# Layer 0 of a conv-attention kernel: rows in blocks of 1024 by single key tiles, doubled keys, and an output projection in four quadrants of the array

## The chip, the cores and the metric

The kernel runs on one core of one Trainium2 chip. The core has five engines that run side by side, each with its own queue in program order: TensorE (matrix products, PE in the profile, its weight loads PEld), VectorE (DVE), ScalarE (ACT), GpSimd (POOL) and SyncE (SP), from which most DMA transfers are issued. Engines wait for each other by semaphores. TensorE writes to PSUM[...]; the other operands lie in SBUF.

The metric is the device time of one launch, in microseconds, the median of several runs. Less is better. A profiled execution has a span, from its first to its last instruction; the time of a run is a little more than the span.

## The reference

The input x is 4 images of 128 channels and 64x64 places, so 4 batches of N = 4096 tokens of 128 channels. Two layers follow each other:

```
# layer 0, per batch; xf is (128, 4096), m = 64
q, k, v = wq @ xf, wk @ xf, wv @ xf          # each (64, 4096)
att = softmax(k.T @ q, axis=2)               # 4096 x 4096, no mask
x = x + wo @ (att @ v.T).T                   # residual

# layer 1 on tokens t (4096, 128)
h = layernorm(t)
q, k, v = h @ Wq, h @ Wk, h @ Wv             # 128 wide
t = t + softmax(causal(q @ k.T / sqrt(128))) @ v
# then a recurrent feed-forward step over tokens, with a norm, added to t
```

All arithmetic is in float32. The change lies in layer 0; layer 1 matters because it follows layer 0 of the same batch and shares engines and buffers with it.

## The kernel before

**Sizes.** P = 128, BLK = 512 rows (NB = 8 blocks a batch), TPB = 4 tiles of 128 in a block, NT = 32 key tiles, M = 64, B = 4 batches.

**Items.** The attention of both layers is one list of items (`items`), in the order batch, layer, block, pair of key tiles. "Rows" are what the softmax is taken for; "keys" are the other side. For each item `scores` multiplies keys by rows into `s_ps` (128 keys on partitions, two tiles of 512 rows side by side) and ScalarE takes the exp into `p`; `sums` adds `p` to `dsum` on VectorE (the denominators, still spread over partitions); `values` multiplies `v` by `p` and accumulates in `acc` over the block. There are two `s_ps` buffers, four `p` buffers and one `acc`. Values follow scores by two items (`SKEW`), so TensorE alternates: scores of item s, values of item s-2.

**Layer 0 before.** An item is two key tiles, t and t+16, for one block of 512 rows, 16 items a block and 128 a batch. The contraction is only 64 long, so each product uses a quarter of TensorE's array: tile t from partitions 0 to 63, tile t+16 from 64 to 127, and each in two halves of 64 keys. The four run at once. For this the rows of a block must lie on both halves of the partitions: `cols0` projects block m and block m+4 into `kr` (q on one half of the partitions, k on the other) and copies the k half to the other partitions, into `swap`, by DMA. `values` does likewise: partitions 0 to 63 of `acc` get the sum over tiles t, partitions 64 to 127 that over t+16, in two banks for the two halves of the keys in a tile.

When a block ends (`it.last`), ScalarE copies `acc` to `half`, VectorE adds its two banks to `agg` (kept in `xhT`), still with two partial sums on the two halves of the partitions; VectorE adds the two halves of `dsum` to `den`.

**Leaving layer 0.** A block's `agg` is not projected at once but at a visit. At the end of the blocks named in `visits`, `leave` issues the output projection `o_ps` on TensorE: four products 128x128x128 a block with `wo2`, which holds wo twice, so that the contraction over 128 partitions also adds the two partial sums. Then a chain of steps, each due some items later, follows: `joined` (four `xs` on VectorE: o_ps times the reciprocal denominator plus the residual), `moments` (statistics of the layernorm), `norm` and `by_channels` (VectorE transposes, then transfers through DRAM that bring the block into channel layout, `xhT`). The chain of denominators (`folded`: VectorE transpose `sq`, reduction `part`, a transfer through DRAM; then `denominators`) starts at the block's end. All chains wait in one list, and one step is done per item; layer 1's chains wait in the same list.

```
visits = [{2: (0, 1), 4: (2, 3), 6: (4,), 7: (5,)}, {2: (6,), 3: (7,)}]
```

This reads: after block 2 of layer 0 the blocks 0 and 1 leave, after 4 the blocks 2 and 3, after 6 block 4, after 7 block 5; after blocks 2 and 3 of layer 1 the blocks 6 and 7.

**The pool "m".** `misc` hands out PSUM banks from a pool of two buffers (`ps_m`). The output projections `o_ps` of both layers take from it, and so do the projected rows of layer 1 (`r_ps`, in `rows1`), the keys and values of the next batch (`kr_ps`, `v_ps`), and others. A buffer comes free when the last reader of its tile is done; for `o_ps` that is the fourth `xs` of `joined`. At the end of a block `rows()` prepares the rows of the block after next: in layer 0 this takes no instruction, in layer 1 it is an `r_ps`. Before the change `rows()` stands ahead of the visit's projections.

**Order.** The program is written in the order above, and a scheduler then orders each engine's instructions by its own estimates of when they are ready. What comes out is a fixed order on each engine; a waiting instruction holds back all that stand behind it on its engine.

In layer 1, two key tiles of 128x128 products make an item, blocks of 512 rows are causal (block g has 2g+2 items), and the array is used whole. Going from products of 64 rows to products of 128 and back is thus what happens around each `o_ps` and `r_ps` in layer 0.

Of the kernel before, what the change touches and what calls it, by code (L numbers as in the profile page):

```python
# [15 lines left out]
P = 128  # L16
# [343 lines left out]
def fast_path(  # L360
# [63 lines left out]
    for m in range(NB // 2):  # L424
        for g in (m, m + NB // 2):
            nc.sync.dma_start(out=xs[:, 0, ts(g, BLK)], in_=x[0, :, ts(g, BLK)])
# [55 lines left out]
    with tc.tile_pool(name="batch", bufs=1) as batch, tc.tile_pool(name="rows", bufs=2) as rowp, tc.tile_pool(  # L482
# [41 lines left out]
        def cols0(b, m):  # L524

            bt = bs[b]
            if m == 0:
                bt.kr = batch.tile([P, 2, N // 2], F32, tag="kr", name="kr")  # L530
                bt.swap = batch.tile([P, N // 2], F32, tag="swap", name="swap")
                bt.v = batch.tile([P, NT // 2, 2, M], F32, tag="v", name="v0")
            for h, w in enumerate((wqk, wkq)):
                ps = misc("kr_ps")
                nc.tensor.matmul(ps, lhsT=w, rhs=xs[:, b, ts(m + h * NB // 2, BLK)], start=True, stop=True)  # L535
                if h:
                    nc.scalar.copy(bt.kr[:, h, ts(m, BLK)], ps)
                else:
                    nc.vector.tensor_copy(bt.kr[:, h, ts(m, BLK)], ps)
                rows, keys = slice(M - h * M, P - h * M), slice(h * M, h * M + M)  # L540
                nc.sync.dma_start(out=bt.swap[keys, ts(m, BLK)], in_=bt.kr[rows, h, ts(m, BLK)])

        def vals0(b, m):

            ps = misc("v_ps")
            for h in range(2):
                nc.tensor.matmul(  # L547
                    ps[h * M : h * M + M], lhsT=wv0, rhs=xs[:, b, ts(m + h * NB // 2, BLK)], start=True, stop=True
                )
            if b:  # L550

                sq = wk.tile([P, Q * TPB, S], F32, tag="sqv", name="sqv")
                nc.vector.transpose(
                    out=sq.rearrange("p (q j) r -> p q j r", q=Q), in_=ps.rearrange("p (j q t) -> p q j t", q=Q, t=S)
                )
                by_t = dram2.tile([S, Q, TPB, Q, S], F32, tag="by_t", name="by_t")
                for c in range(Q):
                    nc.sync.dma_start(out=by_t[:, :, :, c].rearrange("t q j r -> t (q j) r"), in_=sq[ts(c, S)])
                for q in range(Q):
                    nc.sync.dma_start(  # L560
                        out=bs[b].v[ts(q, S), ts(m, TPB)].rearrange("t j h c -> t (j h c)"),
                        in_=by_t[:, q].rearrange("t j c r -> t (j c r)"),
                    )
                return
            vT = wk.tile([P, BLK], F32, tag="vT", name="vT")
            nc.scalar.copy(vT, ps)
            return vT
# [7 lines left out]
        def rows0(b, g):  # L575

            h, m = g // (NB // 2), g % (NB // 2)
            bt = bs[b]
            half = [bt.swap, bt.swap]
            half[1 - h] = bt.kr[:, h]  # L580
            bt.next.append([half[i][i * M : i * M + M, ts(m, BLK)] for i in range(2)])
# [56 lines left out]
        def projected(layer, agg):  # L638

            op = misc("o_ps")  # L640
            for j in range(TPB):
                nc.tensor.matmul(  # L642
                    op[:, ts(j, P)], lhsT=agg[:, ts(j, P)], rhs=wv1 if layer else wo2, start=True, stop=True
                )
            return op

# [72 lines left out]
        def finish0(b, g):  # L719

            agg, den = bs[b].agg, bs[b].den
            mem = []

            def norm():
                if g == 0:
                    bs[b].xh = batch.tile([P, NT, P], F32, tag="xh", name="xh")
                normed(b, g, bs[b].xh[:, ts(g, TPB)], *mem.pop())

            def by_channels():
                sq = squares(bs[b].xh[:, ts(g, TPB)])  # L730
                by_r = dram2.tile([S, Q, TPB, Q, S], F32, tag="by_r", name="by_r")
                for q in range(Q):
                    nc.sync.dma_start(
                        out=by_r[:, :, :, q].rearrange("r c j t -> r (c j) t"),
                        in_=sq[ts(q, S)].rearrange("r c j t -> r (c j) t"),
                    )
                for c in range(Q):
                    nc.sync.dma_start(
                        out=bs[b].xhT[ts(c, S), ts(g, BLK)], in_=by_r[:, c].rearrange("r j q t -> r (j q t)")
                    )  # L740

            def first():
                own = folded(den, False)
                mem.append(own)

            def leave(late):

                op = projected(0, agg)

                def rest():  # L750
                    yield 1 + late, lambda: (joined(0, b, g, op), mem.append(moments(b, g)))
                    yield 1, norm
                    yield 2, by_channels

                return rest()

            bs[b].leave[g] = leave
            yield 1, first
            yield 9, lambda: denominators(0, b, g, mem[0])

        def finish1(b, g):
# [12 lines left out]
            def first():  # L774
# [4 lines left out]
                joined(1, b, g, projected(1, agg))  # L779
# [91 lines left out]
        def block(layer, b, g, pairs):  # L871
            blocks.append((layer, b, g))
            for k, tiles in enumerate(pairs):
                it = Item()
                it.layer, it.b, it.g, it.tiles = layer, b, g, tiles
                it.first, it.last = k == 0, k == len(pairs) - 1
                items.append(it)

        for b in range(B):
            for g in range(NB):  # L880
                block(0, b, g, [((t, 0, BLK), (t + NT // 2, 0, BLK)) for t in range(NT // 2)])
# [5 lines left out]
        def scores(it):  # L887
# [3 lines left out]
            off = 0  # L891
            it.at = []
            for h, (t, q0, n) in enumerate(it.tiles):
                if it.layer == 0:

                    part = slice(h * M, h * M + M)
                    for c in range(2):
                        nc.tensor.matmul(  # L898
                            ps[c * M : c * M + M, off : off + n],
                            lhsT=bs[it.b].kr[part, h, ds(t % (NT // 2) * P + c * M, M)],  # L900
                            rhs=rows[h],
# [3 lines left out]
                else:  # L905
                    lhsT, rhs = bs[it.b].xhT[:, ts(t, P)], rows[:, q0:]
                    nc.tensor.matmul(ps[:, off : off + n], lhsT=lhsT, rhs=rhs, start=True, stop=True)  # L907
                it.at.append((t, q0, n, off))
                off += n
            it.p = prob.tile([P, 2 * BLK], F32, tag="p", name="p")  # L910
            if it.layer == 0:
                nc.scalar.activation(it.p[:, :off], ps[:, :off], AF.Exp, bias=nshift)  # L912
            else:
# [14 lines left out]
        def sums(it):  # L928
# [4 lines left out]
            if all(n == BLK for _, _, n, _ in it.at):  # L933
# [14 lines left out]
        def values(it):  # L948
# [4 lines left out]
            for h, (t, q0, n, o) in enumerate(it.at):  # L953
                if it.layer == 0:

                    for r in range(2):
                        part = slice(r * M, r * M + M)
                        nc.tensor.matmul(  # L958
                            bt.acc[h * M : h * M + M, r],
                            lhsT=bt.v[part, t % (NT // 2), t // (NT // 2)],  # L960
                            rhs=it.p[part, o : o + n],
                            start=it.first,
                            stop=it.last,
                        )
                else:
# [7 lines left out]
            if it.last:  # L973
                if it.layer == 0:
# [3 lines left out]
                    bt.agg = bt.xhT[:, ts(it.g, BLK)]  # L978
                    half = wk.tile([P, 2, BLK], F32, tag="half", name="half")
                    nc.scalar.copy(half, bt.acc)  # L980
                    nc.vector.tensor_tensor(bt.agg, half[:, 0], half[:, 1], ALU.add)
                else:
# [6 lines left out]
                bt.den = wk.tile([P, BLK], F32, tag="den", name="den")  # L989
                nc.vector.tensor_tensor(bt.den, it.den[:, 0], it.den[:, 1], ALU.add)  # L990

        waiting = []


        visits = [{2: (0, 1), 4: (2, 3), 6: (4,), 7: (5,)}, {2: (6,), 3: (7,)}]
        assert NB == 8

        def push(slot, chain):
            step = next(chain, None)
            if step:  # L1000
                waiting.append((slot + step[0], step[1], chain))
# [23 lines left out]
        def tokens():  # L1025

            while started:
                b, g = started.pop(0)
                tokens0(b, g)
# [25 lines left out]
        for s in range(len(items) + SKEW + 16):  # L1055
# [5 lines left out]
            if 0 <= s - SKEW < len(items):  # L1061
                it = items[s - SKEW]
                values(it)
                if it.last:
                    rows()
                    tokens()
                    for k, g in enumerate(visits[it.layer].get(it.g, ())):
                        push(s, bs[it.b].leave[g](8 * k))
                    push(s, (finish1 if it.layer else finish0)(it.b, it.g))
            if s < len(items):  # L1070
                sums(items[s])
            due = [w for w in waiting if w[0] <= s]
            if due:
                w = min(due, key=lambda w: w[0])
                waiting.remove(w)
                w[1]()
                push(s, w[2])
            elif side:
# [5 lines left out]
        assert not waiting and not side  # L1084
# [215 lines left out]
```

## Time and profile before

| | us |
|---|---|
| median of 3 runs | 2052.87 |
| lowest, highest | 2051.19, 2055.78 |
| span of the profiled execution | 2050.8 |
| TensorE busy in it | 2036.7 |
| VectorE busy | 1484.8 |
| ScalarE busy | 988.4 |

The profiled execution is one more execution beside those runs; its span lies 2.1 us under the median of the runs. The four batches are alike: each takes 491.5 us from one first visit to the next (o_ps at 110.33, 601.84, 1093.34 and 1583.90 us, the last after a slightly different end of layer 1), some 220 us of it items of layer 0.

The costliest groups of layer 0 (line, engine, operation, tiles and shapes, count, busy time, mean length in ns of one, idle time of the engine before them):

```profile
L938 DVE TENSOR_TENSOR dsum<-dsum,p 128x1024 f32<-128x1024 f32 x676 | 826.3, 1222 | 429.1 <-ACT p L914 308.3
L912 ACT ACTIVATE p<-s_ps,nshift 128x1024 f32<-128x1024 f32 x512 | 569.7, 1117 | 316.7 <-PE s_ps L898 309.8
L958 PE MATMUL acc<-p,v 64*64 64x512 f32 x4096 | 542.9, 590 | 0.0
L898 PE MATMUL s_ps<-swap,kr 64*64 64x512 f32 x2048 | 538.9, 591 | 0.9 <-ACT p L912 0.9
L898 PE MATMUL s_ps<-kr 64*64 64x512 f32 x2048 | 524.9, 591 | 0.0
L652 DVE SCALAR_TENSOR_TENSOR xs<-o_ps,recs,xs 128x128 f32<-128x128 f32 x256 | 74.5, 341 | 3.3 <-PE o_ps L642 0.3
```

A float32 product shows as two matmul instructions, each with its weight load. Products in different quarters of the array overlap, so the busy time of a group is less than its count times its mean. The matmuls' ends are modelled; their starts are the better measure.

### The profile page before, as it was taken

Reading aid. Unit: us, or ns where it says so; the run is one execution under the profiler, and the core shown is the slowest. Engines: PE = TensorE matmul, PEld = TensorE weight load, DVE = VectorE, ACT = ScalarE, POOL = GpSimd, SP = SyncE. Lnnn points to the kernel's source line nnn. Section 1 sums busy time; section 2 is a strip of 40 time slices with the busy share of each in tenths; the row PEclk is TensorE's granted clock in tenths of the full one; section 3 lists DMA queues with packets and bytes.
Section 4 is the critical chain, followed back from the end, with each engine's and each line's share of the span. In section 5 each row is a group of like instructions: output and inputs, shape, how many; then the busy total and the mean of one; then the engine's idle time right before and its main releaser. Section 6 shows DMA issues by size and latency. Waiting matters only on the chain.

```text
span 2050.8 us, 30808 instructions
## 1 busy us (share of the span) xinstructions
PE 2036.7 (99%) x11646; PEld 909.9 (44%) x11646; DVE 1484.8 (72%) x2862; ACT 988.4 (48%) x1071; POOL 137.9 (7%) x237
## 2 busy tenths in 40 slices
PE   9999999999999999999999999999999999999998
PEld 3643354444333345444433335444433334544456
DVE  4799877555889987555588997654578998765567
ACT  4666632323666653332466663333356665333346
POOL 1000011000000011000000001100000000100004
PEclk9999999999999999999999999999999999999999
DMA  3111021231201112223111001123000110210046
GB/s 88 53 33 28 12 42 37 51 79 37 58 2 23 22 22 43 47 62 67 21 53 22 17 18 42 37 64 86 16 17 2 22 23 12 52 43 21 18 107 237
DMA packets 238445, 89.03 MB, mean 43 GB/s; under 512 B 174816, under 2 KB 219360, under 8 KB 237776
## 3 DMA queue, kind: packets, MB, share of 16 engines
q1 hardware_dynamic: 237280, 86.42, 17.8%
q8 instruction: 93, 1.52, 0.3%
q14 instruction: 64, 0.52, 0.1%
q0 software_dynamic: 288, 0.39, 0.1%
q10 hardware_dynamic: 720, 0.16, 0.0%
HBM read 45.84 MB, written 36.89 MB: 40 GB/s over the span
## 4 chain that ended last, share of the span: by engine, by line
PE 96%; DVE 2%; ACT 2%; issue 0%; POOL 0%; ACTq 0%; POOLq 0%
PE s_ps L907 22%; PE acc L966 22%; PE s_ps L898 22%; PE acc L958 21%; PE o_ps L642 3%; PE r_ps L595 1%; PE kr_ps L535 1%; PE wx_ps L838 1%; DVE z L1166 1%; PE v_ps L547 1%; ACT y L1170 1%; DVE xr L1202 0%; PE warm_ps L496 0%; ACT xs L1170 0%; ACT early L1170 0%
## 5 line engine op out<-in xcount | busy, mean ns | idle before, releaser
L938 DVE TENSOR_TENSOR dsum<-dsum,p 128x1024 f32<-128x1024 f32 x676 | 826.3, 1222 | 429.1 <-ACT p L914 308.3
L912 ACT ACTIVATE p<-s_ps,nshift 128x1024 f32<-128x1024 f32 x512 | 569.7, 1117 | 316.7 <-PE s_ps L898 309.8
L914 ACT ACTIVATE p<-s_ps 128x1024 f32<-128x1024 f32 (+2 forms) x288 | 274.5, 953 | 609.2 <-PE s_ps L907 604.8
L958 PE MATMUL acc<-p,v 64*64 64x512 f32 x4096 | 542.9, 590 | 0.0
L898 PE MATMUL s_ps<-swap,kr 64*64 64x512 f32 x2048 | 538.9, 591 | 0.9 <-ACT p L912 0.9
L898 PE MATMUL s_ps<-kr 64*64 64x512 f32 x2048 | 524.9, 591 | 0.0
L907 PE MATMUL s_ps<-rows,xhT 128*128 128x512 f32 (+3 forms) x1152 | 502.9, 559 | 0.0
L966 PE MATMUL acc<-p,xh 128*128 128x512 f32 (+3 forms) x1152 | 500.9, 557 | 0.0
L966 PEld LDWEIGHTS acc<-p,xh 128*128 128x128 f32 x1152 | 216.3, 190 | 244.3 <-issue 234.2
L907 PEld LDWEIGHTS s_ps<-rows,xhT 128*128 128x128 f32 x1152 | 214.0, 190 | 243.3 <-issue 203.4
L958 PEld LDWEIGHTS acc<-p,v 64*64 64x64 f32 x4096 | 166.6, 133 | 272.5 <-issue 251.6
L898 PEld LDWEIGHTS s_ps<-swap,kr 64*64 64x64 f32 x2048 | 151.4, 133 | 131.0 <-issue 107.8
L898 PEld LDWEIGHTS s_ps<-kr 64*64 64x64 f32 x2048 | 140.7, 133 | 138.0 <-issue 133.8
L666 POOL TENSOR_TENSOR ln_rstd<-ln_var,mhalf 128x4 f32<-128x4 f32 x64 | 68.2, 1066 | 1099.3 <-DVE ln_var L664 1099.3
L946 DVE TENSOR_TENSOR dsum<-dsum,p 128x256 f32<-128x256 f32 (+1 forms) x120 | 55.4, 497 | 64.4 <-POOL p L918 64.4
L652 DVE SCALAR_TENSOR_TENSOR xs<-o_ps,recs,xs 128x128 f32<-128x128 f32 x256 | 74.5, 341 | 3.3 <-PE o_ps L642 0.3
L682 DVE TENSOR_SCALAR xh<-xs,ln_mv,ln_rstd 128x128 f32<-128x128 f32 x252 | 70.3, 342 | 2.1
L918 POOL TENSOR_SCALAR_AFFINE_SELECT p<-p 128x128 f32<-128x128 f32 x128 | 36.1, 306 | 486.1 <-ACT p L914 473.7
L661 DVE BATCH_NORM_STATS2 ln_st<-xs 128x6 f32<-128x128 f32 x256 | 63.3, 270 | 0.0
L936 DVE COPY dsum<-p 128x1024 f32<-128x1024 f32 x60 | 41.0, 683 | 14.7 <-ACT p L914 10.8
L843 ACT COPY xs<-wx_ps 128x512 f32<-128x512 f32 x31 | 18.1, 585 | 65.6 <-DVE stats L839 63.6
L606 DVE STREAM_TRANSPOSE sq<-den 128x512 f32<-128x512 f32 x64 | 45.4, 709 | 1.7
(148 smaller groups left out, 991.7 us busy)
## 6 DMA issues: line engine op xcount, KB each, us to landing
xs<-in_xT SPq DMA_DIRECT2D x32, 256.0 KB, 3.0
by_r<-sqT SPq DMA_DIRECT2D x128, 64.0 KB, 2.2
xhT<-by_r SPq DMA_DIRECT2D x128, 64.0 KB, 2.0
by_c<-sqT SPq DMA_DIRECT2D x124, 64.0 KB, 1.8
xhT<-by_c SPq DMA_DIRECT2D x31, 256.0 KB, 2.7
xs<-in_x SPq DMA_DIRECT2D x12, 512.0 KB, 5.8
swap<-kr SPq DMA_DIRECT2D x32, 128.0 KB, 2.3
x2c<-sqT SPq DMA_DIRECT2D x64, 64.0 KB, 2.3
```

The lines of the kernel that those rows point to most:

```text
L642: nc.tensor.matmul(op[:, ts(j, P)], lhsT=agg[:, ts(j, P)], rhs=wv1 if layer else wo2, start=True, stop=True)
L652: nc.vector.scalar_tensor_tensor(t, in0=op[:, ts(j, P)], scalar=rec[:, j : j + 1], in1=t, op0=ALU.mult, op1=ALU.add)
L661: nc.vector.bn_stats(st[:, j], xs[:, b, ds(g * BLK + j * P, P)])
L666: nc.gpsimd.tensor_tensor(y, var, mhalf, ALU.pow)
L682: nc.vector.tensor_scalar(dst[:, j], xs[:, b, ds(g * BLK + j * P, P)], mv[:, j, 0:1], y[:, j : j + 1], ALU.subtract, ALU.mult)
L898: nc.tensor.matmul(ps[c * M : c * M + M, off : off + n], lhsT=bs[it.b].kr[part, h, ds(t % (NT // 2) * P + c * M, M)], rhs=rows[h], start=True,
L907: nc.tensor.matmul(ps[:, off : off + n], lhsT=lhsT, rhs=rhs, start=True, stop=True)
L912: nc.scalar.activation(it.p[:, :off], ps[:, :off], AF.Exp, bias=nshift)
L914: nc.scalar.activation(it.p[:, :off], ps[:, :off], AF.Exp, scale=float(P) ** -0.5)
L938: nc.vector.tensor_tensor(flat, flat, it.p, ALU.add)
L958: nc.tensor.matmul(bt.acc[h * M : h * M + M, r], lhsT=bt.v[part, t % (NT // 2), t // (NT // 2)], rhs=it.p[part, o : o + n], start=it.first ...
L966: nc.tensor.matmul(bt.acc[:, 0, q0:], lhsT=bt.xh[:, t], rhs=it.p[:, o : o + n], start=it.first and h == 0, stop=it.last and h == 1,)
```

## The change

Layer 0 is cut the other way. An item is now one key tile for 1024 rows (two blocks, a pair), 32 items a pair, 4 pairs and 128 items a batch. The rows of block 2m lie on one half of the partitions, those of block 2m+1 on the other, as they come out of `cols0`; now the keys must lie on both halves, and `swap` holds the second copy of the q half instead of the k half. An item still has four products at once for the scores and four for the values. `acc` holds one block of the pair on each half of its partitions, and `agg` so has two blocks of 64 channels; nothing is left to add over partitions. `dsum` holds the two blocks side by side, so `den` is not formed in layer 0.

The projection of a pair, `projected0`, is 16 products of 64x64x128: for each of four column tiles, two blocks (r) by two halves of 64 tokens (c), into two `o_ps`. A visit is one pair. The chain is split into more steps (`joined` and `moments` apart), layer 0 and layer 1 have lists of their own, so that a step of each can be done per item, and the visit now stands ahead of `rows()`.

```
-            for h, w in enumerate((wqk, wkq)):
+            for h, w in enumerate((wkq, wqk)):
                 ps = misc("kr_ps")
-                nc.tensor.matmul(ps, lhsT=w, rhs=xs[:, b, ts(m + h * NB // 2, BLK)], start=True, stop=True)
+                nc.tensor.matmul(ps, lhsT=w, rhs=xs[:, b, ts(2 * m + h, BLK)], start=True, stop=True)
...
         def rows0(b, g):
-            half = [bt.swap, bt.swap]
-            half[1 - h] = bt.kr[:, h]
-            bt.next.append([half[i][i * M : i * M + M, ts(m, BLK)] for i in range(2)])
+            bs[b].next.append([bs[b].kr[r * M : r * M + M, r, ts(g, BLK)] for r in range(2)])
+
+        def keys0(b, t, r):
+            h, m, j = t // TPB % 2, t // TPB // 2, t % TPB
+            bt, part, at = bs[b], slice(r * M, r * M + M), ds((m * TPB + j) * P, P)
+            return bt.swap[part, at] if r == h else bt.kr[part, h, at]
...
-        def projected(layer, agg):
+        def projected0(agg):
+            ops = [misc("o_ps") for _ in range(2)]
+            for j in range(TPB):
+                for r in range(2):
+                    part = slice(r * M, r * M + M)
+                    for c in range(2):
+                        nc.tensor.matmul(
+                            ops[r][c * M : c * M + M, ts(j, P)],
+                            lhsT=agg[part, ds(j * P + c * M, M)],
+                            rhs=wo2[part],
+                            start=True,
+                            stop=True,
+                        )
+            return ops
...
-        def finish0(b, g):
+        def finish0(b, pair):
...
+                yield 1, lambda: joined(0, b, g, op)
+                yield 1 + 4 * (g % 2), lambda: mem.append(moments(b, g))
+                yield 1, norm
+                yield 2, by_channels
+            def leave():
+                ops = projected0(agg)
+                return [joining(2 * pair + k, op) for k, op in enumerate(ops)]
+            bs[b].leave[pair] = leave
+            yield 1, lambda: first(0)
+            yield 2, lambda: first(1)
+            yield 6, lambda: [denominators(0, b, 2 * pair + k, own[k]) for k in range(2)]
...
-                block(0, b, g, [((t, 0, BLK), (t + NT // 2, 0, BLK)) for t in range(NT // 2)])
+            for g in range(NB // 2):
+                block(0, b, g, range(NT))
...
+                for r in range(2):
+                    keys = keys0(it.b, it.tile, r)
                     for c in range(2):
                         nc.tensor.matmul(
-                            ps[c * M : c * M + M, off : off + n],
-                            lhsT=bs[it.b].kr[part, h, ds(t % (NT // 2) * P + c * M, M)],
-                            rhs=rows[h],
+                            ps[c * M : c * M + M, ts(r, BLK)],
+                            lhsT=keys[:, ts(c, M)],
+                            rhs=rows[r],
...
                         nc.tensor.matmul(
-                            bt.acc[h * M : h * M + M, r],
-                            lhsT=bt.v[part, t % (NT // 2), t // (NT // 2)],
-                            rhs=it.p[part, o : o + n],
+                            bt.acc[c * M : c * M + M, r],
+                            lhsT=bt.v[part, m * TPB + j, h],
+                            rhs=it.p[part, ts(c, BLK)],
...
-        visits = [{2: (0, 1), 4: (2, 3), 6: (4,), 7: (5,)}, {2: (6,), 3: (7,)}]
+        visits = [{1: 0, 2: 1, 3: 2}, {2: 3}]
...
                 if it.last:
+                    if it.g in visits[it.layer]:
+                        for chain in bs[it.b].leave[visits[it.layer][it.g]]():
+                            push(s, 0, chain)
                     rows()
                     tokens()
-                    for k, g in enumerate(visits[it.layer].get(it.g, ())):
-                        push(s, bs[it.b].leave[g](8 * k))
-                    push(s, (finish1 if it.layer else finish0)(it.b, it.g))
+                    push(s, it.layer, (finish1 if it.layer else finish0)(it.b, it.g))
...
-            due = [w for w in waiting if w[0] <= s]
-            if due:
-                w = min(due, key=lambda w: w[0])
-                waiting.remove(w)
-                w[1]()
-                push(s, w[2])
-            elif side:
+            busy = False
+            for layer in range(2):
+                due = [w for w in waiting[layer] if w[0] <= s]
+                if due:
+                    busy = True
+                    w = min(due, key=lambda w: w[0])
+                    waiting[layer].remove(w)
+                    w[1]()
+                    push(s, layer, w[2])
+            if side and not busy:
```

The input of the first batch is loaded in the order of its blocks (before: 0, 4, 1, 5 and so on), and the token-layout input `xs<-in_xT` is loaded two blocks at a time. Layer 1, the end of the program and the numbers of buffers stay as they are.

## The prediction

> **What bounds the kernel now.** I read the page from the top: busy shares, then the chain of waits, then what TensorE waited for, then the timeline of one place where layer 0 is projected.
>
> ```profile
> PE 2036.7 (99%) x11646; PEld 909.9 (44%) x11646; DVE 1484.8 (72%) x2862; ACT 988.4 (48%) x1071; POOL 137.9 (7%) x237
> PE 96%; DVE 2%; ACT 2%; issue 0%; POOL 0%; ACTq 0%; POOLq 0%
> ```
>
> TensorE is busy 99% of the span and is 96% of the chain: a change counts only by what it adds to or takes from TensorE's queue. What TensorE waited for says the same; the longest waits are at the start and at the end (columns: waiting, released by, us in total, times, longest):
>
> ```profile
> PE warm_ps L496 <- POOL ident masks.py:199: 2.6, 1, 2.6
> PE tp L1232 <- DVE total L1230: 1.1, 1, 1.1
> PE s_ps L898 <- ACT p L912: 0.9, 2, 0.5
> ```
>
> So there is no idle time to win, and a new wait on TensorE is paid in full. The timeline of TensorE where block 2 of layer 0 ends and blocks 0 and 1 are projected (start, length, line, tile, count):
>
> ```profile
> 109.15 1.25 PE L958 MATMUL acc<-p,v 64*64 64x512 f32 x8
> 110.33 2.05 PE L642 MATMUL o_ps<-wo,xhT 128*128 128x128 f32 x16
> 112.32 0.65 PE L898 MATMUL s_ps<-swap,kr 64*64 64x512 f32 x2
> 112.33 0.65 PE L898 MATMUL s_ps<-kr 64*64 64x512 f32 x2
> 112.80 0.59 PE L898 MATMUL s_ps<-swap,kr 64*64 64x512 f32 x2
> 112.81 0.60 PE L898 MATMUL s_ps<-kr 64*64 64x512 f32 x2
> 113.23 1.04 PE L958 MATMUL acc<-p,v 64*64 64x512 f32 x8
> 114.08 0.60 PE L898 MATMUL s_ps<-swap,kr 64*64 64x512 f32 x2
> ```
>
> A product is two instructions. In the trace four 64x64 instructions, one for each quadrant of the array, start within 0.02 us and the next four 0.429 us later. An item of layer 0 has eight products, so four such groups: 1.716 us. VectorE at the same place:
>
> ```profile
> 107.32 1.23 DVE L938 TENSOR_TENSOR dsum<-dsum,p 128x1024 f32<-128x1024 f32 x1 [0.50 <-ACT p L912]
> 108.58 0.69 DVE L990 TENSOR_TENSOR den<-dsum 128x512 f32<-128x512 f32 x1
> 109.30 0.71 DVE L606 STREAM_TRANSPOSE sq<-den 128x512 f32<-128x512 f32 x1
> 110.05 0.69 DVE L608 TENSOR_REDUCE part<-sq 128x16 f32<-128x512 f32 x1
> 110.65 0.68 DVE L936 COPY dsum<-p 128x1024 f32<-128x1024 f32 x1
> 111.44 1.23 DVE L938 TENSOR_TENSOR dsum<-dsum,p 128x1024 f32<-128x1024 f32 x1
> 112.59 0.35 DVE L652 SCALAR_TENSOR_TENSOR xs<-o_ps,recs,xs 128x128 f32<-128x128 f32 x1
> ```
>
> The lines to keep: o_ps is written at 110.33 to 112.3 and its first reader on VectorE comes 5.3 us after the block's last exp (end 107.29). An o_ps buffer is held that long. Today nothing on TensorE asks for it meanwhile.
>
> [...]a visit with sixteen 128-row instructions 0.112 us apart (1.79 us) delays the next exp by 2.14 us, so going into 128 rows and back costs 0.35 us.[...]
>
> **The change, part by part.** All sums are against the profiled span, 2050.8 us; the median of the runs is 2052.87, 2.1 us above.
>
> Main loop: still 512 items of eight products in groups of four, other quadrants in another order (both orders occur today at 0.429 us): 128 x 1.716 us a batch, unchanged: 0. Single key tiles ask for the second half of the keys later at the start: 0, since TensorE doesn't wait for the first. Key copies in place of row copies: the same 32 transfers on SP, 2.3 us each to land and far from their use but for the first, which the first scores await today too: 0. Moved on SP and POOL: the eight transfers a block that turn xh round, one pow (1.07 us), the token loads two blocks at a time, and the next batch's x, let go after 32 items instead of 16. Their users come at least an r_ps later: 12 slots at the nearest (layer 1 block 4, over 25 us) against two hops of about 2 us: 0. The denominators' five transfers have ten items of cover: 0. Half as many half<-acc copies (1.01 us) and agg additions, no den addition in layer 0: some 6 us less on VectorE a batch, off the path: 0. The block ends without a projection cost TensorE nothing today (110.33 to the next visit at 167.41 is 32 items and one visit), so halving them saves nothing.
>
> Projection, today, per batch: two visits of two blocks, 2 x 2.14, and four of one block beside an r_ps that changes mode anyway, 4 x 8 x 0.112 = 0.89 each: 7.84 us.
>
> After: sixteen products of 64x64x128, two instructions each: 8 groups of four. The trace has no such group. Below: 128 columns at the rate of 0.429/512 are 0.107, 0.86 a visit.[...] I take 0.95: a 128-column product already starts every 0.112, bursts of eight instructions appear within 0.055[...]. Four visits a batch, in the order in which the changed program's instructions stand:
>
> Visit A, end of pair 1: no mode change, 0.95. VectorE: after the last dsum of a pair come two transposes and two reductions, and the eight xs and most moments stand between three dsum; by the spacings of the rows above its lag behind the exp grows to 4.8 us, and at the 12th item to 6.0 (today at most 4.2). The exp of item k+4 reuses the p buffer of item k, so a lag of 4 x 1.716 - 1.12 - 1.23 - 0.06 = 4.45 is free; and exps may be 1.15 late (118.02 to 119.23, less 0.06) before TensorE misses an s_ps buffer. 6.0 - 5.6 leaves about 0.45 us of stall. Together 1.4.
>
> Visit B, end of pair 2: now the projection stands ahead of the r_ps (rows of layer 1, block 0), where today r_ps came first. Its order on TensorE (line, tile, count):
>
> ```
> L973 acc<-p,v x4
> L653 o_ps<-wo,xhT x16
> L913 s_ps<-kr,swap x2
> L913 s_ps<-kr x1
> L596 r_ps<-xhT,g
> L913 s_ps<-kr x1
> ```
>
> and on VectorE dsum x19, sq x2, part x2, dsum copy, dsum, agg (xhT<-half), xs x8. The two o_ps take both buffers of the pool "m"; r_ps asks for one, and waits for the fourth xs of the first. VectorE, from the end of the pair's last exp, with the start-to-start spacings of the trace (dsum 1.26 to a reader of its result and 1.14 to another, transpose 0.64, reduction 0.60, copy 0.79, agg 0.60, xs 0.26): dsum 0.03, transpose 1.29, second 1.93, reductions 2.57 and 3.17, copy 3.77, dsum 4.55, agg 5.69, xs 6.29, fourth xs ends 7.41. TensorE: values end 2.94, o_ps 3.9, three of the four quadrants of the next scores 4.8; then r_ps, which stands before the fourth, waits until 7.45: stall 2.65. Behind it wait the fourth product, all later scores and so every exp. The broken group costs 0.86 more. Together 0.95 + 2.65 + 0.86 = 4.46.
>
> Visit C, the step into layer 1, on the profile's time axis (first batch): o_ps, then acc waits for half (ACT copies it from 255.3 to 256.3; o_ps ends at 256.05): 0.3. Then r_ps again waits for the xs: VectorE there is at den until 256.7, two transposes, agg, xs from 258.6, fourth ends 259.7; TensorE would be ready at 258.3: 1.46. The second r_ps waits for the eighth xs, 260.8, just when TensorE comes. Less 0.28 for the mode change around r_ps that is gone: 2.43.
>
> Visit D, in layer 1, block 2: changes into 64 rows and back, taken as the same 0.35: 1.3, and 0.1 of waiting, as an item of scores (1.7) stands before r_ps. 1.4.
>
> Sum 9.7 against 7.84: 1.85 us a batch, 7.4 in four. 2050.8 + 7.4 + 2.1 = 2060.3.
>
> What each unknown bounds: [...] If at 0.86: -0.7. If A's lag stalls nothing and half is in time: -3.0.
>
> **Rivals.** (1) The waits are not there: r_ps gets its buffer as it comes. Then 7.84 stands against 4 x 0.95 + 0.35 + 0.86 = 5.0: 2.8 a batch, 11.3 us faster, 2041.5. For it: VectorE has less to do. Against: the order is fixed, and today's first xs also comes 5.3 us after the exp. It ends on the faster side once A, B and C together wait less than 1.8 us a batch instead of 4.9. (2) The waits are half as long: -0.6 a batch, 2050.5, no change. (3) [...] (4) [...]
>
> **How the numbers follow.** Forecast 0.60, its own range 2056 to 2065; (1) 0.12; (2) 0.10; (3) 0.11; (4) 0.07. A measurement of this kernel can tell about 0.2% (4.1 us) from no change. Slower by more: the forecast but for its low end (0.57), (3) and (4): 0.75. Same: (2) and that end: 0.13. Faster: (1), 0.12. To leave out no more than 2 in 10 the range covers the forecast, (3), (4) and part of (2): 2053 to 2069.
>
> **What would show it.** A wait of r_ps on xs of some 2.6 us, four times, in the list of TensorE's waits, and of some 1.5 four times more; the sixteen o_ps within about 1 us; dsum lags above 4.5 us after visit A; block ends elsewhere at the old pace. Wrong if r_ps does not wait, if TensorE's busy time falls by over 10 us at the same idle time, or if the groups of four are no longer 0.429 us apart.

## The result and the profile after

The changed kernel takes 2058.02 us (median of 12 runs, 2057.13 to 2059.30) against 2052.30 us (12 runs, 2051.19 to 2055.78): ratio 1.0028, 95% interval 1.0019 to 1.0036. It is slower, by 5.7 us in the median; the forecast was 2060.3, with a range of 2053 to 2069. The profiled execution has a span of 2055.4 us, 4.6 more than before; its time, 2057.13, is the lowest of the twelve, so the stretches below explain these 4.6 us and not the whole 5.7.

The first two parts of the page after, busy time by engine and the chain by engine:

```profile
PE 2026.6 (99%) x11902; PEld 912.4 (44%) x11902; DVE 1454.5 (71%) x2814; ACT 976.1 (47%) x1055; POOL 139.8 (7%) x237
PE 92%; DVE 4%; ACT 2%; issue 1%; POOL 0%; DVEq 0%; POOLq 0%; ACTq 0%
```

TensorE is busy 10.1 us less and still the span grew: 14.7 us of new idle time. In the chain TensorE has fallen from 96% to 92%, VectorE has risen from 2% to 4% and issue from 0 to 1%. What TensorE waited for names the place (waiting, released by, us in total, times, longest):

```profile
PE r_ps L596 <- issue: 10.4, 4, 2.6
PE r_ps L596 <- PE acc L982: 3.9, 4, 1.0
PE warm_ps L495 <- POOL ident masks.py:199: 2.6, 1, 2.6
```

Eight waits of r_ps, two a batch, are nearly all of it (14.3 us). "issue" means that the profile shows no releaser; "PE acc" is only what came last in TensorE's own queue. Who released r_ps is seen when both engines are laid side by side. First TensorE at the end of pair 2 in batch 0 (start, length, line, tile, count):

```profile
192.96 1.06 PE L653 MATMUL o_ps<-wo,xhT 64*64 64x128 f32 x32
193.83 0.60 PE L913 MATMUL s_ps<-kr,swap 64*64 64x512 f32 x2
193.85 0.59 PE L913 MATMUL s_ps<-kr 64*64 64x512 f32 x1
194.26 0.60 PE L913 MATMUL s_ps<-kr,swap 64*64 64x512 f32 x2
194.28 0.59 PE L913 MATMUL s_ps<-kr 64*64 64x512 f32 x1
197.45 1.10 PE L596 MATMUL r_ps<-xhT,g 128*128 128x512 f32 x2 [2.58 <-issue]
198.48 0.74 PE L913 MATMUL s_ps<-kr 64*64 64x512 f32 x1
198.48 0.77 PE L973 MATMUL acc<-p,v 64*64 64x512 f32 x3
```

Then VectorE:

```profile
190.06 1.22 DVE L953 TENSOR_TENSOR dsum<-dsum,p 128x1024 f32<-128x1024 f32 x1 [0.49 <-ACT p L920]
191.32 1.31 DVE L607 STREAM_TRANSPOSE sq<-dsum 128x512 f32<-128x512 f32 x2
192.55 1.24 DVE L609 TENSOR_REDUCE part<-sq 128x16 f32<-128x512 f32 x2
193.70 0.68 DVE L951 COPY dsum<-p 128x1024 f32<-128x1024 f32 x1
194.49 1.23 DVE L953 TENSOR_TENSOR dsum<-dsum,p 128x1024 f32<-128x1024 f32 x1
195.63 0.68 DVE L997 TENSOR_TENSOR xhT<-half 128x512 f32<-128x512 f32 x1
196.23 2.15 DVE L667 SCALAR_TENSOR_TENSOR xs<-o_ps,recs,xs 128x128 f32<-128x128 f32 x8
```

Eight xs in 2.15 us, 0.26 apart, beginning at 196.23: the fourth, the last reader of the first o_ps, ends near 197.4, and r_ps starts at 197.45. VectorE has no gap from 191.3 on. TensorE starts nothing behind r_ps in the meantime: the fourth product of the scores follows at 198.48. The 32 small instructions of o_ps take 0.87 us (192.96 to 193.83), 0.11 for a group of four.

The next table tells where the 4.6 us come from. For each item I took the start of its first product of scores in the trace after, less the same in the trace before; a cell is what this difference grows by in that stretch (items counted from 0 in a batch; 128 is the first of layer 1). The last row runs to the end of the program in batch 3, and the sum of batch 0 holds the time before its item 0. The forecast column is the prediction's own sum.

| stretch | batch 0 | 1 | 2 | 3 | forecast |
|---|---|---|---|---|---|
| before item 0 of batch 0 | -0.54 | | | | 0 |
| items 0 to 22 | -0.61 | -0.88 | -0.88 | -0.01 | 0 |
| 22 to 51: a visit less | -1.75 | -2.14 | -2.14 | -2.14 | -2.14 |
| 51 to 85: visit A for a visit of two blocks | -1.05 | -0.89 | -0.89 | -1.23 | 1.40 - 2.14 = -0.74 |
| 85 to 128: visit B for a visit of one | +5.14 | +3.45 | +3.45 | +3.45 | 4.46 - 0.89 = +3.57 |
| 128 to 140: visit C for a visit of one | +1.53 | +1.53 | +1.53 | +1.53 | 2.43 - 0.89 = +1.54 |
| rest of layer 1: visit D for two | -0.55 | -0.54 | -0.24 | -0.53 | 1.40 - 1.78 = -0.38 |
| sum | +2.17 | +0.53 | +0.83 | +1.07 | +1.85 each |

Three things stand out: a gain of 0.88 in two batches that was put at zero, 1.7 us more in batch 0 than elsewhere at visit B, and otherwise about the forecast. The 0.61 of batch 0 in the first stretch is no gain: before, items 18 and 19 took this much longer than two others, and now items 34 and 35 do, behind the end of the first pair and so in the next stretch. Why they do was not looked into.

### The profile page after: what moved, and what is told of

The parts are those of the page before. It is cut to its first block, busy times and chain, and to the rows that moved or that the text cites. A ratio compares the mean times of both kernels' runs of the same rounds, so it can differ in the third digit from the quotient of the medians.

```text
span 2055.4 us, 31316 instructions
## 1 busy us (share of the span) xinstructions
PE 2026.6 (99%) x11902; PEld 912.4 (44%) x11902; DVE 1454.5 (71%) x2814; ACT 976.1 (47%) x1055; POOL 139.8 (7%) x237
## 4 chain that ended last, share of the span: by engine, by line
PE 92%; DVE 4%; ACT 2%; issue 1%; POOL 0%; DVEq 0%; POOLq 0%; ACTq 0%
PE s_ps L926 22%; PE acc L982 22%; PE s_ps L913 20%; PE acc L973 20%; PE o_ps L643 1%; PE r_ps L596 1%; DVE dsum L953 1%; PE kr_ps L534 1%; PE wx_ps L854 1%; DVE z L1188 1%; PE v_ps L546 1%; ACT y L1192 1%; PE o_ps L653 0%; DVE xr L1224 0%; ACT p L920 0%
## 5 line engine op out<-in xcount | busy, mean ns | idle before, releaser
L953 DVE TENSOR_TENSOR dsum<-dsum,p 128x1024 f32<-128x1024 f32 x692 | 845.6, 1222 | 462.2 <-ACT p L929 289.5
L973 PE MATMUL acc<-p,v 64*64 64x512 f32 x4096 | 643.4, 591 | 0.0
L913 PE MATMUL s_ps<-kr,swap 64*64 64x512 f32 x2048 | 585.8, 591 | 0.3
L913 PE MATMUL s_ps<-kr 64*64 64x512 f32 x2048 | 580.2, 591 | 0.0
L973 PEld LDWEIGHTS acc<-p,v 64*64 64x64 f32 x4096 | 205.1, 133 | 260.5 <-issue 239.9
L913 PEld LDWEIGHTS s_ps<-kr,swap 64*64 64x64 f32 x2048 | 165.3, 133 | 137.9 <-issue 119.2
L913 PEld LDWEIGHTS s_ps<-kr 64*64 64x64 f32 x2048 | 163.3, 133 | 130.7 <-issue 120.3
L951 DVE COPY dsum<-p 128x1024 f32<-128x1024 f32 x44 | 30.2, 686 | 28.9 <-ACT p L929 25.6
L596 PE MATMUL r_ps<-xhT,g 128*128 128x512 f32 x64 | 33.6, 607 | 14.2 <-issue 10.4
```

What stands on the lines that cost most here:

```text
L913: nc.tensor.matmul(ps[c * M : c * M + M, ts(r, BLK)], lhsT=keys[:, ts(c, M)], rhs=rows[r], start=True, stop=True,)
L953: nc.vector.tensor_tensor(flat, flat, it.p, ALU.add)
L973: nc.tensor.matmul(bt.acc[c * M : c * M + M, r], lhsT=bt.v[part, m * TPB + j, h], rhs=it.p[part, ts(c, BLK)], start=it.first, stop=it.last,)
```

## The experiments

Spans are compared with 2055.4 (changed kernel) and 2050.8 (before); the medians with a median of before taken beside them. The time before item 0 is 0.8 us less to 0.7 us more than in the trace before, in kernels that all start as the changed one does, so differences of span of that size are read from the items instead.

**1. rows() ahead of the visit.**

```diff
+                    rows()
+                    tokens()
                     if it.g in visits[it.layer]:
                         for chain in bs[it.b].leave[visits[it.layer][it.g]]():
                             push(s, 0, chain)
-                    rows()
-                    tokens()
```

> The changed kernel with one edit: at a block end r_ps (rows for layer 1) is issued ahead of the visit's o_ps products, as it was before the change. Theory (r_ps waits for the o_ps buffers that VectorE holds): the wait of r_ps on issue of 2.6 us at the end of pair 2 is gone in all four batches, the broken groups of four with it (0.9 us, paid at the step into layer 1), and the stretch of 3.4 us at half clock in batch 0 (1.7 us). In its place o_ps waits some 0.6 us for ScalarE, which copies half and then rows before the second r buffer is free. The second r_ps of the step into layer 1 now gets the first o_ps buffer, so about half of the wait there stays. Sum: some 2.9 us a batch at the end of pair 2, 0.3 to 1 at the step, 1.7 once: 13 to 17 us, span 2039 to 2042. Rival (the wait is only handed on: o_ps waits for r_ps as long as r_ps waited for o_ps): span 2052 to 2056, and a wait of o_ps of over 2 us.

Measured: span 2042.2, median 2043.92 of 5 runs, ratio to before 0.996 (0.9946 to 0.9974). In the list of waits no line of r_ps is left. TensorE at the end of pair 2 in batch 1:

```profile
682.12 1.13 PE L596 MATMUL r_ps<-xhT,g 128*128 128x512 f32 x2
683.18 1.54 PE L653 MATMUL o_ps<-wo,xhT 64*64 64x128 f32 x26
684.51 0.60 PE L913 MATMUL s_ps<-kr,swap 64*64 64x512 f32 x2
684.55 0.49 PE L653 MATMUL o_ps<-wo,xhT 64*64 64x128 f32 x6
```

o_ps now takes 1.33 us to the next scores instead of 0.87, about 0.5 more. The expectation puts this at ScalarE's copy of rows; the view doesn't show what released it. The wait was not handed on at its old length. That is 13.2 us less than the changed kernel, at the low edge of the 13 to 17 expected, and the span is 0.2 above the range given for it. The rest of layer 1 with visit D, where nothing waited, lost 0.42 to 0.65 a batch by the same reordering. One edit of order, with the same work, puts the kernel on the other side of before: the order is the cause of the loss.

**2. The folding of the denominators three slots later**, and pinned there in program order, so that VectorE has a shorter queue ahead of the xs while TensorE's order stays as it is there.

```diff
-            nc.vector.transpose(out=sq.rearrange("p j q s -> p (j q s)"), in_=den)
+            keep(nc.vector.transpose(out=sq.rearrange("p j q s -> p (j q s)"), in_=den))
...
-            yield 1, lambda: first(0)
+            yield 4, lambda: first(0)
```

> The changed kernel with the transposes and reductions of a pair's denominators three slots later on VectorE, in the program's order; TensorE's order at the end of pair 2 is as in the changed kernel. Theory (the length of r_ps' wait is VectorE's queue up to the fourth xs): without two transposes and two reductions that queue is bound by the exps: copy at 1.75 after the pair's last exp, dsum 3.46, agg 4.60, xs 5.20, the fourth ends 6.3 in place of 7.45. r_ps' wait falls from 2.6 to some 1.5 us in each batch; no half clock in batch 0 (1.7 us); the stall at the 13th item after the end of pair 1 goes (0.2 to 0.3). Span 2048 to 2050. Rival (r_ps waits for something else than VectorE, its weights or its keys): wait unchanged at 2.6, span 2054 to 2056.

Measured: span 2058.2, median 2060.13 of 5, ratio 1.0038 (1.0023 to 1.0052). First TensorE at the end of pair 2 in batch 0, then three lines from the list of waits:

```profile
198.44 1.10 PE L596 MATMUL r_ps<-xhT,g 128*128 128x512 f32 x2 [1.60 <-issue]
```

```profile
PE r_ps L596 <- issue: 10.9, 8, 1.6
PE s_ps L913 <- ACT p L920: 3.4, 5, 0.8
PE r_ps L596 <- PE s_ps L926: 2.5, 4, 0.8
```

The wait at B fell from 2.58 to 1.60, where VectorE's queue said 1.5: its length is that queue. The sum is a miss by 8 us and more. The work was only moved: after visit A it now stands behind the xs, ahead of and between the layernorm's small refining steps (ln_z) and transposes, where VectorE was late already, and TensorE lost 0.95 to 1.65 us more there in each batch; at D r_ps came to wait as well (0.6 to 0.8). These outweigh 1.0 a batch won at B. It also shows a batch 0 without the extra 1.7.

**3. r_ps one item ahead of the block's end.**

```diff
+                if it.layer == 0 and it.tile == NT - 2:
+                    rows()
                 if it.last:
...
-                    rows()
+                    if it.layer:
+                        rows()
```

> The changed kernel with r_ps issued one item ahead of the end of pairs 2 and 3, so that it neither follows o_ps nor stands ahead of it; in layer 1 it stays behind the visit. Theory: no wait at the end of pair 2, r_ps costs its 0.86 and a change of mode (0.3), o_ps 0.86: 3.4 us a batch less than the changed kernel, 1.7 once for the clock, and at the step into layer 1 the wait for half and that of r_ps go too (up to 1.5 us a batch). Span 2034 to 2040, below the first experiment. Rival (wait handed on): 2050 or more.

Measured: span 2033.1, median 2035.83 of 4, ratio to before 0.992 (0.9904 to 0.9937). The same place in batch 1:

```profile
678.07 1.13 PE L596 MATMUL r_ps<-xhT,g 128*128 128x512 f32 x2
679.12 0.65 PE L913 MATMUL s_ps<-kr,swap 64*64 64x512 f32 x2
...
680.89 1.05 PE L653 MATMUL o_ps<-wo,xhT 64*64 64x128 f32 x32
681.76 0.60 PE L913 MATMUL s_ps<-kr,swap 64*64 64x512 f32 x2
```

r_ps costs 1.05 and o_ps 0.87, no wait on either. 5.06 us a batch less than the changed kernel, and in batch 0 another 1.7. All of the change's parts are in this kernel; only r_ps stands elsewhere. So the change with r_ps placed there is worth 17.7 us of span on before (2050.8 to 2033.1), and as it was made it kept none of that. Not all of it is the projection: 0.8 lie before item 0, 2.4 in items 0 to 22. What the earlier r_ps alone would do to the kernel before was not tried.

**4. Before, with the last wx_ps of a batch one slot sooner**, to see where the 0.88 of batches 1 and 2 comes from.

```diff
-            yield 1 if final else 6 if g < 2 or g == NB - 1 else 4, third
+            yield 1 if final else 6 if g < 2 else 5 if g == NB - 1 else 4, third
```

> The kernel before, with the last wx_ps of each batch one slot sooner (5 in place of 6). Theory: the 0.88 us that the change gains at the start of batches 1 and 2 is a collision in the kernel before: VectorE's den of block 0 stands ahead of the moments of wx_ps, ScalarE's copy of wx_ps waits 3.1 us for them with two exps behind it, and TensorE waits for one of them. One slot sooner there is no such wait, as in batch 3: span 2049.1 (1.76 less), no wait of s_ps L898 on p of 0.5 at 546 and 1038. Rival (each block end without a projection costs 0.88 somewhere): span 2050.8, same waits.

The place in the kernel before, batch 1, ScalarE, and the product of TensorE that waited:

```profile
544.90 0.59 ACT L843 COPY xs<-wx_ps 128x512 f32<-128x512 f32 x1 [3.13 <-DVE stats L839]
545.39 2.12 ACT L912 ACTIVATE p<-s_ps,nshift 128x1024 f32<-128x1024 f32 x2
547.39 1.02 ACT L980 COPY half<-acc 128x1024 f32<-128x1024 f32 x1
```

```profile
546.56 0.65 PE L898 MATMUL s_ps<-swap,kr 64*64 64x512 f32 x2 [0.46 <-ACT p L912]
```

Measured: span 2049.3, one run of 2051.0, so the times alone decide nothing and the items do. The wait of s_ps on p is gone; batches 1 and 2 each gain 0.53, not 0.88, and batch 3 loses 0.16 (0.31 more was won before item 0, which the edit doesn't touch). ScalarE's copy still waits (2.79 us), now without the block's end right behind it. So 0.53 of the 0.88 is the collision of wx_ps with the end of block 0, which the change removes by having no block end there. The other 0.35 stays open.

**5. A longer wait.** Three reductions more on VectorE ahead of the xs of pair 2.

```diff
+                for k in range(3):
+                    src = den[:, k % 2].rearrange("p (n s) -> p n s", s=S)
+                    tc.keep_in_program_order(nc.vector.tensor_reduce(t[:, k], src, AX.X, ALU.add))
...
             def leave():
+                if pair == 1:
+                    pad()
                 ops = projected0(agg)
```

> The changed kernel with three reductions of 0.60 us more on VectorE ahead of the first xs at the end of pair 2 (their sum goes into rec times zero, so nothing else changes). In the program r_ps now stands behind the whole of the next scores and three of the four next values. Theory (the half clock of batch 0 comes from the length of the wait): r_ps' idle time grows from 2.6 to about 3.8 us, which is 1.0 us more a batch net of the two groups that now go ahead, 4 in all; and the clock falls to half for some 3.4 us after it in more batches than one, 1.7 us each: span 2061 (two) to 2065 (four), with spans that differ between executions by steps of about 1.7. Rival (the half clock of batch 0 has another cause and stays in batch 0): 2059.4. Rival (it was chance and does not come back): 2057.7.

Measured: span 2066.1, median 2067.48 of 4, ratio 1.0073 (1.0058 to 1.0089). The line of waits, and the table of stretches right after r_ps in batches 0 to 3 (stretch, its length, busy time of PE, PEld, DVE, ACT, POOL, granted clock, DMA share, GB/s):

```profile
PE r_ps L596 <- issue: 15.7, 4, 3.9
```

```profile
202.60:206.00 3.40, 3.40 (x25) 1.22 (x28) 2.45 (x18) 1.05 (x2) 1.01 (x1) 0.70 0.02 5
697.00:700.40 3.40, 3.40 (x21) 1.09 (x24) 2.72 (x19) 0.77 (x2) 1.01 (x1) 0.63 0.00 0
1191.00:1195.00 4.00, 4.00 (x21) 1.18 (x24) 3.39 (x21) 0.71 (x2) 1.01 (x1) 0.57 0.02 4
1686.00:1690.00 4.00, 4.00 (x21) 1.19 (x24) 3.29 (x21) 0.81 (x2) 1.01 (x1) 0.57 0.02 4
```

With a wait of 2.6 us the granted clock fell in one batch of four (to 0.50 for 3.41 us), with 3.9 in all four (0.57 to 0.70 over the stretches above), with the 1.6 of the second experiment in none (0.999 over its whole span, as before the change). That is the extra 1.7 us of batch 0: from item 85 to 128 this kernel takes 1.28 us longer than the changed one in batch 0, where both have a slow stretch, and 2.98 in the others, where only this one has; the difference is 1.70, half of 3.4.

Why one batch of four, when all four waits are equally long? In the changed kernel the clock is 0.50 from 198.89 to 202.30 us, for 3.41 us. So I cut its trace into stretches of this length, counted from there (batch 0, then batch 1; same columns):

```profile
195.48:198.89 3.41, 1.44 (x6) 0.51 (x10) 3.41 (x14) 0.31 (x1) 0.00 (x0) 1.00 0.12 5
198.89:202.30 3.41, 3.41 (x20) 1.07 (x16) 2.44 (x13) 1.39 (x2) 1.01 (x1) 0.50 0.02 2
687.00:690.41 3.41, 1.58 (x34) 0.70 (x26) 3.31 (x6) 1.08 (x2) 0.00 (x0) 1.00 0.12 4
690.41:693.83 3.42, 2.65 (x18) 0.96 (x22) 3.42 (x22) 1.10 (x2) 0.14 (x1) 1.00 0.10 8
```

In batch 0 most of the wait falls into one stretch, which is left 1.97 us idle (3.41 less 1.44), and the next one runs at 0.50. In batch 1 the same wait is split between two stretches, 1.83 and 0.77 idle, and the clock stays at 1.00. Of batches 2 and 3 the emptiest stretch has 1.31 and 1.68 us idle, and the clock stays at 1.00 there too. Whether the place of the wait decides is not shown by this: only one of the four was followed by a slow stretch, and no run moved a wait of 2.6 us. As the ends of matmuls are modelled, the idle times are approximate.

The steps of 1.7 between executions did not show (spans 2065.2 to 2066.5), as four of four leave no room for them. 1.25 of the 10.6 us more than the changed kernel lie before item 0 and have nothing to do with the edit; without them the span is 2064.8, inside the 2061 to 2065 expected.

**6. Experiment 3 with the second xs of pairs 1 and 2 later**, pinned eight slots behind its old place.

```diff
-                yield 1, lambda: joined(0, b, g, op)
-                yield 1 + 4 * (g % 2), lambda: mem.append(moments(b, g))
+                late = g % 2 and pair < 2
+                yield 9 if late else 1, lambda: joined(0, b, g, op, late)
+                yield 1 + 4 * (g % 2) * (not late), lambda: mem.append(moments(b, g))
```

> The third experiment's kernel with the second xs of pairs 1 and 2 eight slots later on VectorE, so that its lag behind the exps stays under 4.5 us. Theory (the 0.2 to 0.4 us that TensorE loses at the 13th to 18th item after the end of pair 1 is that lag: the exps find no free p buffer): these losses are gone, 0.9 us in all, span 2032.2 beside 2033.1; no exp waits for dsum in layer 0. Rival (the loss there is something else, ScalarE for instance): 2033.1, the loss stays.

ScalarE in the changed kernel, in batch 0 after visit A, then the same exps in this one:

```profile
159.72 1.12 ACT L920 ACTIVATE p<-s_ps,nshift 128x1024 f32<-128x1024 f32 x1 [0.60 <-PE s_ps L913]
162.56 1.11 ACT L920 ACTIVATE p<-s_ps,nshift 128x1024 f32<-128x1024 f32 x1 [1.71 <-DVE dsum L953]
```

```profile
161.54 1.11 ACT L923 ACTIVATE p<-s_ps,nshift 128x1024 f32<-128x1024 f32 x1 [0.60 <-PE s_ps L916]
163.26 1.11 ACT L923 ACTIVATE p<-s_ps,nshift 128x1024 f32<-128x1024 f32 x1 [0.60 <-PE s_ps L916]
```

Measured: span 2033.0, median 2035.01 of 5 runs, ratio 0.9914 (0.9901 to 0.9928). Against experiment 3, TensorE's items gain 0.22, 0.40, 0.38 and 0.05 us over this stretch in the four batches, about 1.05 in all where 0.9 was expected; the span itself, less than 0.2 shorter, hides most of it: this execution began 0.4 later, lost 0.2 elsewhere in batch 0 and 0.3 at its very end. The lag of VectorE behind the exps is the cause of the loss after A. It fell less than meant, to 4.7 us (5.1 in batch 1) instead of below 4.5, and 6 exps of layer 0 still wait for dsum (4.7 us in all; in experiment 3 it was 30, for 22.8), without a loss on TensorE. In the timed runs the two kernels can't be told apart; both are faster than before and than the changed kernel.

## Why the prediction was right

The mechanism was the forecast one, and its largest term was right. That the sum came as near as it did is partly luck: the clock, which the forecast left out, made up for most of a gain that it had put at zero.

- **r_ps waits for the buffers of o_ps**: right, and to the place. Forecast at B: r_ps 7.45 us after the pair's last exp, a stall of 2.65. Measured in batch 0: the exp ends at 190.03, r_ps starts at 197.45, 7.42 later; TensorE is idle for 2.58 to 2.60 in all four batches. Experiments 1 and 3 take it away by order alone, 2 and 5 change it by what is added to or taken from VectorE's queue.
- **Visit B in all**: +3.57 forecast, +3.45 measured in three batches. One term was right in size but not in place: the broken group of four (0.86). After r_ps, three instructions of acc started beside the fourth product of the scores (acc x3 at 198.48), so nothing was lost there; items 85 to 128 pay it at the far end, ahead of the 128x128 products of layer 1: the difference grows by 0.83 between items 115 and 128, and by nothing there in experiment 3, where no group is broken.
- **Visit C**: 1.54 forecast, 1.53 measured, but with other parts, so that the agreement is luck: r_ps waits 0.97 instead of 1.46, acc starts 0.54 behind the o_ps (their 0.87 taken off) instead of 0.3, of which the profile shows 0.35 as a wait for half, and the 0.28 to be saved on the change of mode doesn't show.
- **Visit A**: 1.40 forecast, 1.25 measured in batches 1 and 2 (0.87 of products, 0.38 of lag), 1.09 and 0.91 in the others. The lag reached 5.9 us in batches 1 and 2 and 5.6 in the others, against 6.0.
- **The small products**: 0.95 a visit forecast, 0.87 measured where nothing waits. That is 0.11 for a group of four, beside the 0.107 estimated from 0.429 us for 512 columns, so rival 3, small products bound by issue, is out.
- **Visit D**: -0.38 forecast; -0.24 to -0.55 measured. Other visits of layer 1 fall together differently in the two kernels; what of the spread is D was not separated.
- **Zero for fewer block ends**: wrong by 0.88 in two batches of four. The prediction looked at one stretch of batch 0 where block ends cost nothing; at the first block end of batches 1 and 2 a wx_ps of the batch before collides with it (experiment 4, for 0.53 of it; the rest stays open). This is the largest term in the 2.8 us by which the forecast's 7.4 exceeds the span's 4.6.
- **Rival 4, a lower clock after the stall at B in every batch**: half right. It came in one batch of four, for 1.7 us: after 2.58 us of idle in batch 0 the granted clock was 0.50 for 3.41 us, after the 2.58 to 2.60 of the other three it stayed at 1.00.
- **Rivals 1 and 2**: out. The waits are there, at B at their full length (2.6), at C at two thirds of it (0.97 of 1.46). Experiment 3 shows what a kernel without the waits takes: 2035.83, even below the 2041.5 of rival 1.

The 2.8 us in full: 2.0 less in items 0 to 51, 0.5 before item 0, 1.1 for A, 0.4 in layer 1; at B 0.5 less for the wait and the products, and the clock's 1.7 the other way. TensorE's busy time did fall by 10.1 us, which the prediction named as a sign of being wrong, but only at the same idle time; idle time grew by 14.7.

## What to carry to other kernels

When a step takes every buffer of a small pool, find who asks for the next one in the order of issue, and add up the work of the readers' engine to the read that frees it: here the change was worth 17.7 us with that request placed ahead, and all of it was lost with the request behind. Moving the asker ahead of the taker by one item won it back; thinning the readers' queue shortened the wait and lost more elsewhere. A third buffer was not tried. Where TensorE stalls for some us, look at the granted clock behind the stall: here a slow stretch cost 1.7 us more, after one of four waits of 2.6 us and after four of four of 3.9.

## What the runs showed of the hardware that was not expected

- After 2.58 to 2.60 us of idle TensorE the granted clock fell to 0.50 for 3.41 us in one place of four and stayed at 1.00 in three; after 3.9 us it fell in four of four (0.57 to 0.70 over 3.4 to 4.0 us), after 1.6 us in none of four (0.999 over the span). In the changed kernel the 3.41 us ahead of the slow stretch held 1.97 us of idle time; stretches cut at the same distance around the other three waits held at most 1.83.
- With one of the four products of a group held back behind r_ps (batch 1), products of acc started beside those of the scores, from 692.68 on again four instructions every 0.43 us; the 0.83 us lost shows only between items 115 and 128, ahead of the 128x128 products of layer 1.
